# A gated graph network and an attention layer: gates by tanh, scores through DRAM, a product in three float32r passes

## The chip, the core and the metric

The kernel runs on one core of a Trainium2 chip. A core has engines that run their own instruction streams in order and meet at semaphores: TensorE (PE in the profile; its weight loads are PEld), VectorE (DVE), ScalarE (ACT), GpSimd (POOL) and SyncE (SP), which here issues nearly all DMA transfers. The metric is the device time of one execution in microseconds; the time before is the median of five runs.

## The reference

The input x is 64 graphs of 256 nodes with 256 features, adj 64 matrices of 256 x 256. Layer 0 is a gated graph network of three steps, layer 1 a graph attention; each is added to its input.

```python
# layer 0
h = relu(layernorm(x))
A = (adj != 0)
for i in range(3):
    m = h @ weight[i]
    aggr = A.T @ m                       # per graph
    gi, gh = aggr @ w_ih.T + b_ih, h @ w_hh.T + b_hh
    r = sigmoid(i_r + h_r)
    z = sigmoid(i_z + h_z)
    n = tanh(i_n + r * h_n)
    h = (1 - z) * n + z * h
x = x + h
# layer 1
y = relu(layernorm(x))
h = y @ W.T
e = (h @ a_left)[:, :, None] + (h @ a_right)[:, None, :]
e = where(e > 0, e, 0.2 * e)
e = where(adj == 0, -1e9, e)
x = x + softmax(e) @ h
```

All is float32.

## The kernel before

The graphs are worked on in 32 pairs. Most tiles are 128 partitions by 512 elements: one graph's 256 x 256, or one half of the features of both graphs of a pair.

*Setup* (`setup`). The weights are loaded and transposed on TensorE. weight[i] and w_ih are multiplied into one matrix per step. Each factor is cut in two (`factors`, lines 372 to 392): a top part with the low 12 bits of its word masked away (`cut`, line 322, mask -4096), and what is left. Three float32r arrays are kept in `fac`: the top, the remainder times 4096, and a combination (line 387). W^T is kept whole in plain float32 (`wT`). The products a_left W and a_right W are made once (`va`), so that the scores are dot products with y.

*Gates.* The activations are cut in the same way (`split`, lines 445 to 453): a cut on VectorE, a cast on ScalarE (line 449), a difference (line 450) and a combination (line 451) on VectorE. A product is then three float32r passes (`gate`): two in the group "top" (line 464), then ScalarE multiplies the PSUM bank by 1 + 1/4096 ("scale", line 478), then the third pass, "rest" (line 469). Four gate outputs per feature half are made in each step: r (sigmoid, line 599), the h part of n ("nh", with its bias in the scale), its input part ("ni"), and z (sigmoid, line 610). Line 603 is r times nh, line 606 adds ni, line 607 is the tanh, lines 615 to 617 give the new state.

*Between steps.* "prop" (line 584) multiplies by the adjacency in float32r, "prop copy" (line 588) takes it out of PSUM. The state is held transposed; it is turned back by a DMA transpose (line 489) with gathers (line 494), and a copy on ScalarE (`join`, line 502). The last pair does this on TensorE (line 631).

*Attention*, at the end of `pair`. After the second layer norm, line 656 makes the scores with an accumulating scalar_tensor_tensor. The right-hand scores lie one to a partition; TensorE transposes each column, broadcast, so that every partition gets the row of all 256 (line 667, into a PSUM bank). "leaky" (line 671) adds the left-hand score as bias and applies Prelu on ScalarE. A predicated copy (line 674) puts the scores of edges over -1e9, line 676 takes the maximum, and one operation "exps" for both graphs (lines 679 to 687) makes exponentials and their sums. They are transposed (by DMA; the last pair on TensorE, line 700), "mix" (line 714) multiplies y by them in plain float32, "mix copy" (line 718) takes it out, "project" (line 723) multiplies by W^T in plain float32, and line 728 divides by the sums and adds the residual before the store (line 731).

*Order.* Nothing runs as written. `Plan` gathers all operations with a duration (`occ`), a time to the result (`lat`), and what they read and write. `Plan.run` then lays them out one at a time: the one that can start first, ties by a due time (`prio`), moved by the figures in the table `LEAD` (in ns, by operation name). At most four pairs are under way. Buffers come from fixed sets: 28 "full", 32 "round", 12 "small", 8 PSUM "bank". Each engine's queue, SP's with the DMA issues among them, then holds its instructions in that order. The gates' top products take turns (`in_turn`), so that steps of neighbouring pairs alternate.

Of the kernel before, what the change touches and what calls it, by code (L numbers as in the profile page):

```python
# [10 lines left out]
F32 = mybir.dt.float32  # L11
# [16 lines left out]
    "w load": 28000, "w copy": -12000, "w cut": -5000, "w 1": -17000, "w copies": -7000, "G": -9000, "G copy": -5400,  # L28
    "va copy": 4000, "in 0 stats": 5000, "in 1 relu": 10000, "turn copy 0": -11800, "h0 0": 17000, "h0 d": 13000,
    "h1 0": 36000, "prop 0": 11200, "g0 cut": 3000, "g1 cut": 13000, "g1 0": -28000, "r 0 topT": 51000,  # L30
    "r 0 rest": -4300, "r 0": 29000, "ni 0 rest": 46000, "z 0 topF": -48000, "z 0": 11000, "d mul 0": -19000,
    "r 1 topT": -34000, "r 1 rest": -1000, "nh 1 topF": -42000, "nh 1 scale": -38000, "nh 1 rest": 3000,
    "ni 1 topF": -24000, "tanh 1": 10000, "z 1 topF": -61000, "z 1 scale": -112000, "z 1": 6000, "back 0": -36000,
    "hi 0": 28000, "back copy 1": -67000, "hi 1": 52000, "mid 0 stats": -14000, "right 0": -8000,
    "mid 1 eps": -23000, "mid 1 relu": 9000, "dot 1": -31000, "mix 0": -28000, "p copy 1": 40000,
    "project 1": -6000, "turn 1 gather": 2000,
# [16 lines left out]
class Plan:  # L53
# [6 lines left out]
    def __init__(self, window, lead):  # L60
        self.ops, self.slots, self.window, self.pair = [], {}, window, -1
        self.writer, self.readers = {}, {}
        self.due = None
        self.stage = None
        self.lead = lead
        self.keep = {"full": 0, "round": 0}
# [4 lines left out]
    def op(self, name, eng, occ, lat, fn, r=(), w=(), ahead=0, port=False):  # L71
        o = Op()
        o.eng, o.occ, o.lat, o.fn, o.pair, o.seq = eng, occ, lat, fn, self.pair - ahead, len(self.ops)
        o.succs, o.prio, o.end, o.port, o.due = [], None, None, port, self.due
        o.stage, o.name, o.lead = self.stage, name, self.lead.get(name, 0)
        preds, bufs = set(), set()
        for b, ks in r:
            bufs.add(b)
            for k in ks:
                if (b, k) in self.writer:  # L80
                    preds.add(self.writer[b, k])
                self.readers.setdefault((b, k), []).append(o)
        for b, ks in w:
            bufs.add(b)
            for k in ks:
                if (b, k) in self.writer:
                    preds.add(self.writer[b, k])
                preds.update(self.readers.get((b, k), ()))
                self.writer[b, k], self.readers[b, k] = o, []
        preds.discard(o)  # L90
        o.preds, o.wait = list(preds), len(preds)
        for q in preds:
            q.succs.append(o)
        o.bufs = [b for b in bufs if isinstance(b, Buf)]
        for b in o.bufs:
            b.left += 1
        self.ops.append(o)
        return o
# [102 lines left out]
def tile_gated_gnn_then_gat(  # L201
# [34 lines left out]

    nc = tc.nc
    P = 128
# [15 lines left out]
    plan.slot_class("full", [const.tile([P, GN], F32, name=f"full{i}") for i in range(28)])  # L254
# [4 lines left out]
    plan.slot_class("bank", [psum.tile([P, GN], F32, name=f"bank{i}") for i in range(8)])  # L259

# [28 lines left out]
    A512, V512, S512, VP256, C512 = 475, 605, 660, 392, 522  # L289
    CUT = -4096  # L290
# [7 lines left out]
    b_rz = const.tile([P, EB], F32, name="b_rz")  # L298
    b_i = vec[:, 2 * DB : 2 * DB + EB]
# [3 lines left out]
    wT = const.tile([P, DB, D], F32, name="wT")  # L303
# [21 lines left out]
    def setup():  # L325
# [16 lines left out]
        dve("b_rz", 70, lambda: nc.vector.tensor_add(b_rz, b_i, b_h), r=[("vec", ONE)], w=[("b_rz", ONE)])  # L342

# [10 lines left out]
        def transposed(dst, region, blocks):  # L354

            def go_for(c):
# [8 lines left out]
                act("w copy", 140 + n * 110, lambda: nc.scalar.copy(dst(c), pt.t[:, : n * P]), r=[(pt, ONE)], w=[region(c)])  # L365
# [5 lines left out]

        def factors(m, T):

            def one(kb, half):
                f = lambda j: fac[m][:, j, kb, ts(half, H)]
                b, t = T[kb][half], Buf("full")
                src, top = lambda: b.t[:, :H], lambda: t.t[:, :H]
                key = (f"fac{m}", ((kb, half),))
                cut("w cut", top, src, H, [(b, ONE)], [(t, ONE)])
                dve2("w 1", 460, lambda: nc.vector.tensor_sub(src(), src(), top()), r=[(t, ONE)], w=[(b, ONE)])  # L380

                def copies():
                    nc.scalar.copy(f(0), top())
                    nc.scalar.activation(f(1), src(), AF.Copy, scale=SPLIT)

                act("w copies", 800, copies, r=[(b, ONE), (t, ONE)], w=[(f"fac{m}", ((kb, half, 0),))])
                dve2("w d", 510, lambda: nc.vector.scalar_tensor_tensor(f(2), top(), -C, src(), op0=ALU.mult, op1=ALU.add),
                    r=[(b, ONE), (t, ONE)], w=[(f"fac{m}", ((kb, half, 1),))])

            for half in range(2):  # L390
                for kb in range(DB):
                    one(kb, half)
# [4 lines left out]
        def whole(T, blocks):  # L397
            for half in range(2):
                transposed(lambda c, half=half: T[c][half].t[:, :H], lambda c, half=half: (T[c][half], ONE),
                           blocks[3 * half : 3 * half + 3])  # L400
# [4 lines left out]
        whole(whhT, whh_n)  # L405
# [24 lines left out]
        transposed(lambda c: wT[:, c, :], lambda c: ("wT", (c,)), W_n)  # L430
# [11 lines left out]

    WT = [("wT", (0, 1))]
# [11 lines left out]
    def gate(name, e, terms, tops, apart=False, bias=0.0):  # L455
# [22 lines left out]
        act(name + " scale", 575 if "nh" in name else A512, lambda: nc.scalar.activation(bank.t, bank.t, AF.Identity, bias=bias, scale=1.0 + C),  # L478
# [56 lines left out]
    def pair(p):  # L535
        plan.pair = p

# [33 lines left out]
        for i in range(L):  # L571
# [23 lines left out]
            for db in range(DB):  # L595
# [3 lines left out]
                act(f"r {db}", 575, lambda b=r_, k=pr, db=db: nc.scalar.activation(b.t, k.t, AF.Sigmoid, bias=b_rz[:, db : db + 1]),  # L599
                    r=[(pr, ONE), ("b_rz", ONE)], w=[(r_, ONE)])  # L600
                en = 2 * DB + db
                ph = gate(f"nh {db}", en, [("hh", hs)], tops, bias=b_h[:, en : en + 1])
                dve(f"u {db}", V512, lambda u=u, k=ph, b=r_: nc.vector.tensor_mul(u.t, k.t, b.t),  # L603
                    r=[(ph, ONE), (r_, ONE)], w=[(u, ONE)])
# [6 lines left out]
                    b.t, k.t, AF.Sigmoid, bias=b_rz[:, DB + db : DB + db + 1]),  # L611
# [4 lines left out]
                dve2(f"d mul {db}", V512, lambda d=d, b=z_: nc.vector.tensor_mul(d.t, d.t, b.t), r=[(z_, ONE)], w=[(d, ALL)])  # L616
                dve2(f"d add {db}", V512, lambda u=u, d=d: nc.vector.tensor_add(d.t, d.t, u.t), r=[(u, ONE)], w=[(d, ALL)])
# [31 lines left out]
        for g in range(G):  # L649
# [12 lines left out]
            pR = Buf("bank")  # L662

            def right(sm=sm, pR=pR):
                for nb in range(NB):
                    c = 12 + NB + nb
                    nc.tensor.transpose(pR.t[:, ts(nb, P)], sm.t[:, c : c + 1].to_broadcast([P, P]), ident)  # L667

            pe(f"right {g}", 2 * TR, right, r=[(sm, (14, 15))], w=[(pR, ONE)])
            for nb in range(NB):  # L670
                act(f"leaky {g}", 365, lambda b=sc[g], nb=nb, pR=pR, sm=sm: nc.scalar.activation(
                    parts(b)[:, nb, :], pR.t[:, :N], AF.Prelu, bias=sm.t[:, 12 + nb : 13 + nb], alpha=LEAKY_SLOPE),
                    r=[(pR, ONE), (sm, (12 + nb,))], w=[(sc[g], (nb,))])
# [5 lines left out]
        def exps():  # L679
            for g in range(G):  # L680
                s = sms[g].t
                for k in range(NB):
                    nc.scalar.activation(parts(pm_[g])[:, k, :], parts(pm_[g])[:, k, :], AF.Exp, bias=s[:, k : k + 1],  # L683
                                         accum_out=s[:, 4 + k : 5 + k])

        plan.op("exps", "ACT", 4 * 490 + 2600, 4 * 490 + 1300 + 200, exps, r=[(s, ONE) for s in sms],
                w=[(b, ALL) for b in pm_] + [(s, (1,)) for s in sms])

        for g in range(G):
# [28 lines left out]
            act(f"mix copy {g}", A512, lambda ag=ag, pg=pg: nc.scalar.copy(ag.t, pg.t), r=[(pg, ONE)], w=[(ag, ONE)])  # L718

            def project(ag=ag, pv=pv):  # L720
                for ib in range(NB):
                    for db in range(DB):
                        nc.tensor.matmul(pv.t[:, ts(ib, D)], ag.t[:, db * N + ib * P : db * N + (ib + 1) * P],  # L723
                                         wT[:, db, :], start=(db == 0), stop=(db == DB - 1))

            pe(f"project {g}", 4 * MM, project, r=[(ag, ONE)] + WT, w=[(pv, ONE)])
# [41 lines left out]
```

## Time and profile before

| | us |
|---|---|
| median of 5 runs | 2124.22 (2119.61 to 2126.58) |
| the profiled execution | 2124.36 |
| its span in the profile | 2122.6 |

The engines' idle time before groups of their instructions, with what ended most of it, is read from lines such as these (line, engine, operation, shapes, count, then busy time and mean of one in ns, then idle time):

```profile
L607 ACT ACTIVATE full<-full,vec 128x512 f32<-128x512 f32 x192 | 135.6, 723 | 3.6 <-DVE full L606 3.6
L615 DVE TENSOR_TENSOR full<-full,full 128x512 f32<-128x512 f32 x192 | 132.2, 689 | 75.0 <-ACT full L607 71.5
L603 DVE TENSOR_TENSOR full<-bank,full 128x512 f32<-128x512 f32 x192 | 131.7, 686 | 113.5 <-ACT full L599 107.3
```

The 192 are 32 pairs, three steps and two feature halves. A matmul of plain float32 leaves two records. Records of one engine overlap a little, so the cost of one in a row is the distance between starts, and less than its mean. Idle time of an engine that isn't the bottleneck costs nothing.

### The profile page before, as it was taken

The numbers are of one execution on the slowest core, as the hardware profiler recorded it, in microseconds if no ns is written. First come the engines' busy times: TensorE is split into PE (matmuls) and PEld (weight loads), VectorE is DVE, ScalarE is ACT, GpSimd is POOL, SyncE is SP. The second block draws the span as 40 slices with busy tenths as digits, with TensorE's granted clock in tenths as the row PEclk, the third lists the DMA queues.
The fourth block names the chain that finished last, engine by engine and source line by source line (L and its number), as shares of the span: only waits on it lengthen the run. The fifth ranks groups of instructions, "written<-read, shape, count | busy, mean of one in ns | idle before, by whom it ended". The sixth has DMA issues, their size and how long they took to land.

```text
span 2122.6 us, 31090 instructions
## 1 busy us (share of the span) xinstructions
PE 2082.2 (98%) x9737; PEld 1712.0 (81%) x9737; DVE 1779.9 (84%) x4148; ACT 1892.2 (89%) x3255; POOL 142.8 (7%) x198
## 2 busy tenths in 40 slices
PE   8999999999999999999999999999999999999997
PEld 6787888888888888888888888888888888888775
DVE  7788888888888888888888888888888888888775
ACT  7788999999999999998999999999999999999865
POOL 1000000000000000000000000000000000000000
PEclk9999999999999999999999999999999999999998
DMA  3456765556765655766556765556765556665531
GB/s 100 79 101 120 139 119 109 97 112 121 139 117 105 100 115 121 139 118 102 101 115 125 139 118 105 99 115 122 136 119 105 100 113 126 134 118 90 89 58 40
DMA packets 729253, 234.35 MB, mean 110 GB/s; under 512 B 660976, under 2 KB 729088, under 8 KB 729088
## 3 DMA queue, kind: packets, MB, share of 16 engines
q1 hardware_dynamic: 729056, 232.36, 58.3%
q8 instruction: 77, 1.26, 0.3%
q14 instruction: 88, 0.72, 0.1%
q10 hardware_dynamic: 32, 0.01, 0.0%
HBM read 52.96 MB, written 16.78 MB: 33 GB/s over the span
## 4 chain that ended last, share of the span: by engine, by line
PE 82%; ACT 8%; DMA 5%; SPq 3%; DVE 2%; issue 1%; ACTq 0%; DVEq 0%
PE bank L464 41%; PE bank L469 21%; PE bank L584 7%; PE bank L714 6%; PE bank L723 5%; DMA full<-full 4%; SPq L494 3%; ACT full L502 2%; ACT bank L478 1%; ACT round L449 1%; ACT full L683 1%; PE bank L421 1%; PE bank L667 1%; ACT L683 1%; ACT full L588 0%
## 5 line engine op out<-in xcount | busy, mean ns | idle before, releaser
L464 PE MATMUL bank<-round,fac 128*128 128x512 f32 x2304 | 623.6, 399 | 1.9 <-ACT round L449 1.7
L464 PE MATMUL bank<-round,fac_hh 128*128 128x512 f32 x2304 | 617.3, 397 | 3.6 <-ACT round L449 3.6
L464 PEld LDWEIGHTS bank<-round,fac_hh 128*128 128x128 f32 x2304 | 432.6, 189 | 104.6 <-ACT round L449 4.8
L464 PEld LDWEIGHTS bank<-round,fac 128*128 128x128 f32 x2304 | 432.7, 189 | 101.8 <-ACT round L449 2.1
L478 ACT ACTIVATE bank<-bank 128x512 f32<-128x512 f32 x576 | 339.3, 591 | 47.9 <-PE bank L464 43.9
L502 ACT COPY full<-full 128x1024 uint16<-128x1024 uint16 x310 | 363.2, 1172 | 19.9 <-DMA full<-full 15.8
L469 PE MATMUL bank<-round,fac_hh 128*128 128x512 f32 x1152 | 355.6, 398 | 3.8 <-ACT bank L478 3.6
L469 PE MATMUL bank<-round,fac 128*128 128x512 f32 x1152 | 356.2, 395 | 0.6 <-ACT bank L478 0.5
L450 DVE TENSOR_TENSOR round<-full,full 128x512 fp32r<-128x512 f32 x384 | 255.2, 684 | 1.7
L469 PEld LDWEIGHTS bank<-round,fac 128*128 128x128 f32 x1152 | 214.5, 188 | 50.9 <-ACT bank L478 2.8
L469 PEld LDWEIGHTS bank<-round,fac_hh 128*128 128x128 f32 x1152 | 208.3, 189 | 57.8 <-ACT bank L478 17.5
L451 DVE SCALAR_TENSOR_TENSOR round<-round,full 128x512 fp32r<-128x512 f32 x384 | 252.2, 682 | 0.9 <-PE bank L464 0.5
L449 ACT CAST round<-full 128x512 fp32r<-128x512 f32 x384 | 239.1, 630 | 8.6 <-DVE full L322 5.6
L603 DVE TENSOR_TENSOR full<-bank,full 128x512 f32<-128x512 f32 x192 | 131.7, 686 | 113.5 <-ACT full L599 107.3
L524 POOL TENSOR_TENSOR small<-small,nhalf 128x2 f32<-128x2 f32 x128 | 106.1, 838 | 1787.3 <-DVE small L522 1784.9
L584 PEld LDWEIGHTS bank<-round,round 128*128 128x128 f32 x1536 | 205.8, 190 | 17.7 <-DVE round L642 2.7
L584 PE MATMUL bank<-round,round 128*128 128x256 f32 x1536 | 216.7, 287 | 3.4 <-DVE round L642 2.0
L610 ACT ACTIVATE full<-bank,b_rz 128x512 f32<-128x512 f32 x192 | 131.7, 687 | 89.2 <-PE bank L469 89.1
L615 DVE TENSOR_TENSOR full<-full,full 128x512 f32<-128x512 f32 x192 | 132.2, 689 | 75.0 <-ACT full L607 71.5
L322 DVE TENSOR_SCALAR full<-full 128x512 int32<-128x512 int32 (+1 forms) x400 | 163.7, 418 | 17.3 <-ACT full L588 8.8
L616 DVE TENSOR_TENSOR full<-full,full 128x512 f32<-128x512 f32 x192 | 131.8, 688 | 43.0 <-ACT full L610 42.3
L607 ACT ACTIVATE full<-full,vec 128x512 f32<-128x512 f32 x192 | 135.6, 723 | 3.6 <-DVE full L606 3.6
(78 smaller groups left out, 2397.4 us busy)
## 6 DMA issues: line engine op xcount, KB each, us to landing
full<-full SPq DMA_DIRECT2D x496, 128.0 KB, 3.5
x<-in_x_dram SPq DMA_DIRECT2D x64, 256.0 KB, 3.3
adj<-in_adj_dram SPq DMA_DIRECT2D x64, 256.0 KB, 3.1
full<-in_x_dram SPq DMA_DIRECT2D x64, 256.0 KB, 3.3
out_dram<-full SPq DMA_DIRECT2D x64, 256.0 KB, 2.7
full<-full SPq DMA_DIRECT2D x248, 64.0 KB, 2.2
full<-full SPq DMA_TRANSPOSE x310, 3.1
full<-in_L_gnn_w_ih_dram SPq DMA_DIRECT2D x3, 256.0 KB, 3.0
```

What stands on the lines that cost most here:

```text
L322: dve2(name, 60 + n * 0.54, lambda: nc.vector.tensor_scalar(dst().bitcast(I32), src().bitcast(I32), CUT, None, op0=ALU.bitwise_and), r=r, w=w)
L449: act(name + " 0", C512, lambda: nc.scalar.copy(v0.t, t.t), r=[(t, ONE)], w=[(v0, ONE)])
L450: dve2(name + " 1", V512, lambda: nc.vector.tensor_sub(v1.t, v.t, t.t), r=[(v, ALL), (t, ONE)], w=[(v1, ONE)])
L451: dve2(name + " d", V512, lambda: nc.vector.scalar_tensor_tensor(vd.t, v1.t.bitcast(F32), -SPLIT, t.t, op0=ALU.mult, op1=ALU.add), r=[(v1, ...
L464: nc.tensor.matmul(bank.t, f(m, j, kb), b.t, start=(first and n == 0), stop=True, skip_group_check=True)
L469: nc.tensor.matmul(bank.t, f(m, 2, kb), s[kb][2].t, start=False, stop=True, skip_group_check=True)
L478: act(name + " scale", 575 if "nh" in name else A512, lambda: nc.scalar.activation(bank.t, bank.t, AF.Identity, bias=bias, scale=1.0 + C), ...
L502: act(name, 1065, lambda: nc.scalar.copy(dst.t.bitcast(U16).rearrange("p (j n b) -> p j n b", j=2, b=2), src.t.bitcast(U16).rearrange(f"p ...
L584: nc.tensor.matmul(pa.t[:, ts(g, N)], b, parts(A[g])[:, sb, :], start=(n == 0), stop=(n == len(terms) - 1))
L607: act(f"tanh {db}", 615, lambda u=u, en=en: nc.scalar.activation(u.t, u.t, AF.Tanh, bias=b_i[:, en : en + 1]), r=[("vec", ONE)], w=[(u, ONE)])
L615: dve2(f"d sub {db}", V512, lambda u=u, d=d: nc.vector.tensor_sub(d.t, d.t, u.t), r=[(u, ONE)], w=[(d, ALL)])
L616: dve2(f"d mul {db}", V512, lambda d=d, b=z_: nc.vector.tensor_mul(d.t, d.t, b.t), r=[(z_, ONE)], w=[(d, ALL)])
```

## The change

Three parts of the computation are done in another way, and the order is laid out anew with them.

- r and z are made by tanh: sigmoid(v) = (1 + tanh(v/2))/2. The halves go into the weights (the n block of w_hh is halved at setup, with its bias `b_nh`), the scale of the activation (0.5) and `b_rz`. The u product and the last two operations of the state become scalar_tensor_tensor operations.
- The right-hand scores, in all pairs but the last, are written to a row in DRAM and read back to all partitions by two DMAs that SP issues. leaky then reads them from SBUF with a stride of two elements.
- project is made in three float32r passes, with W^T in factors and the mixed activations split as for the gates.

The exps become one operation per graph, there are 26 "full" buffers in place of 28, and `LEAD` has new figures, some for the first or the last pair only.

```diff
     def __init__(self, window, lead):
...
+        self.prefix = ""
...
-        o.stage, o.name, o.lead = self.stage, name, self.lead.get(name, 0)
+        o.stage, o.name, o.lead = self.stage, self.prefix + name, self.lead.get(name, 0)
+        if self.prefix:
+            o.lead += self.lead.get(o.name, 0)
...
-    plan.slot_class("full", [const.tile([P, GN], F32, name=f"full{i}") for i in range(28)])
+    plan.slot_class("full", [const.tile([P, GN], F32, name=f"full{i}") for i in range(26)])
...
+    dram = ctx.enter_context(tc.tile_pool(name="dram", bufs=1, space=bass.MemoryType.DRAM))
+    plan.slot_class("line", [dram.tile([1, N], F32, name=f"line{i}") for i in range(4)])
...
+    LINE, SPREAD = 7500, 5300
...
-    wT = const.tile([P, DB, D], F32, name="wT")
+    fac["W"] = const.tile([P, 3, DB, D], F32R, name="fac_W")
...
+        dve("b_rz half", 70, lambda: nc.vector.tensor_scalar(b_rz, b_rz, 0.5, None, op0=ALU.mult), w=[("b_rz", ONE)])
+        dve("b_nh", 70, lambda: nc.vector.tensor_scalar(b_nh, b_h[:, 2 * DB :], 0.5, None, op0=ALU.mult), r=[("vec", ONE)], w=[("b_nh", ONE)])
...
-        transposed(lambda c: wT[:, c, :], lambda c: ("wT", (c,)), W_n)
+        w_T = [Buf("full") for _ in range(DB)]
+        transposed(lambda c: w_T[c].t[:, :D], lambda c: (w_T[c], ONE), W_n)
+        for c in range(DB):
+            factor("W", w_T[c], D, lambda j, c=c: fac["W"][:, j, c, :], (c,))
...
-                act(f"r {db}", 575, lambda b=r_, k=pr, db=db: nc.scalar.activation(b.t, k.t, AF.Sigmoid, bias=b_rz[:, db : db + 1]),
+                act(f"r {db}", 575, lambda b=r_, k=pr, db=db: nc.scalar.activation(
+                    b.t, k.t, AF.Tanh, bias=b_rz[:, db : db + 1], scale=0.5),
...
-                dve(f"u {db}", V512, lambda u=u, k=ph, b=r_: nc.vector.tensor_mul(u.t, k.t, b.t),
-                    r=[(ph, ONE), (r_, ONE)], w=[(u, ONE)])
+                dve(f"u {db}", S512, lambda u=u, k=ph, b=r_: nc.vector.scalar_tensor_tensor(
+                    u.t, b.t, 1.0, k.t, op0=ALU.add, op1=ALU.mult), r=[(ph, ONE), (r_, ONE)], w=[(u, ONE)])
...
-                    b.t, k.t, AF.Sigmoid, bias=b_rz[:, DB + db : DB + db + 1]),
+                    b.t, k.t, AF.Tanh, bias=b_rz[:, DB + db : DB + db + 1], scale=0.5),
...
-                dve2(f"d mul {db}", V512, lambda d=d, b=z_: nc.vector.tensor_mul(d.t, d.t, b.t), r=[(z_, ONE)], w=[(d, ALL)])
-                dve2(f"d add {db}", V512, lambda u=u, d=d: nc.vector.tensor_add(d.t, d.t, u.t), r=[(u, ONE)], w=[(d, ALL)])
+                dve2(f"d mul {db}", V512, lambda d=d, b=z_: nc.vector.scalar_tensor_tensor(
+                    d.t, b.t, 1.0, d.t, op0=ALU.add, op1=ALU.mult), r=[(z_, ONE)], w=[(d, ALL)])
+                dve2(f"d add {db}", V512, lambda u=u, d=d: nc.vector.scalar_tensor_tensor(
+                    d.t, d.t, 0.5, u.t, op0=ALU.mult, op1=ALU.add), r=[(u, ONE)], w=[(d, ALL)])
...
+            if p < NPAIR - 1:
+                line, pR = Buf("line"), Buf("full")
+                plan.op(f"line {g}", "SP", 420, LINE, lambda line=line, sm=sm: nc.sync.dma_start(
+                    line.t.rearrange("o (q k) -> (o q) k", k=NB), sm.t[:, 12 + NB : 12 + 2 * NB]),
+                    r=[(sm, (14, 15))], w=[(line, ONE)])
+                plan.op(f"right {g}", "SP", 420, SPREAD, lambda line=line, pR=pR: nc.sync.dma_start(
+                    pR.t[:, :N], line.t.to_broadcast([P, N])), r=[(line, ONE)], w=[(pR, ONE)])
+                pr = lambda pR: pR.t[:, :N].rearrange("p (q k) -> p k q", k=NB)
+            else:
...
             for nb in range(NB):
-                act(f"leaky {g}", 365, lambda b=sc[g], nb=nb, pR=pR, sm=sm: nc.scalar.activation(
-                    parts(b)[:, nb, :], pR.t[:, :N], AF.Prelu, bias=sm.t[:, 12 + nb : 13 + nb], alpha=LEAKY_SLOPE),
-                    r=[(pR, ONE), (sm, (12 + nb,))], w=[(sc[g], (nb,))])
+                act(f"leaky {g}", 365, lambda b=sc[g], nb=nb, pR=pR, sm=sm, pr=pr: nc.scalar.activation(
+                    parts(b)[:, nb, :].rearrange("p (k q) -> p k q", k=NB), pr(pR), AF.Prelu, bias=sm.t[:, 12 + nb : 13 + nb],
+                    alpha=LEAKY_SLOPE), r=[(pR, ONE), (sm, (12 + nb,))], w=[(sc[g], (nb,))])
...
-        def exps():
-            for g in range(G):
-                s = sms[g].t
+        for g in range(G):
+            def exps(s=sms[g], m=pm_[g]):
...
-        plan.op("exps", "ACT", 4 * 490 + 2600, 4 * 490 + 1300 + 200, exps, r=[(s, ONE) for s in sms],
-                w=[(b, ALL) for b in pm_] + [(s, (1,)) for s in sms])
+            act(f"exps {g}", 2 * 497, exps, r=[(sms[g], ONE)], w=[(pm_[g], ALL), (sms[g], (1,))])
...
-            def project(ag=ag, pv=pv):
-                for ib in range(NB):
-                    for db in range(DB):
-                        nc.tensor.matmul(pv.t[:, ts(ib, D)], ag.t[:, db * N + ib * P : db * N + (ib + 1) * P],
-                                         wT[:, db, :], start=(db == 0), stop=(db == DB - 1))
-
-            pe(f"project {g}", 4 * MM, project, r=[(ag, ONE)] + WT, w=[(pv, ONE)])
+            cs = split(f"c{g}", ag)
+
+            def project(js, first, cs=cs, pv=pv):
+                for n, (ib, db, j) in enumerate((ib, db, j) for ib in range(NB) for db in range(DB) for j in js):
+                    nc.tensor.matmul(pv.t[:, ts(ib, D)], cs[j].t[:, db * N + ib * P : db * N + (ib + 1) * P],
+                                     fac["W"][:, j, db, :], start=(first and n == 0), stop=True, skip_group_check=True)
+
+            pe(f"project {g}", 8 * PROP, lambda project=project: project((0, 1), True),
+               r=[(cs[0], ONE), (cs[1], ONE), ("facW", ((0, 0), (1, 0)))], w=[(pv, ONE)])
+            act(f"project {g} scale", A512, lambda pv=pv: nc.scalar.activation(pv.t, pv.t, AF.Copy, scale=1.0 + C), w=[(pv, ONE)])
+            pe(f"project {g} rest", 4 * PROP, lambda project=project: project((2,), False),
+               r=[(cs[2], ONE), ("facW", ((0, 1), (1, 1)))], w=[(pv, ONE)])
```

`factor` is the body of `factors` as a function of its own, with the same four operations; it now serves W^T too. `transposed` gets a width up to which it copies, and multiplies the rest by 0.5.

## The prediction

> **What bounds the kernel now.** I read the head of the page first: which engine is never free.
>
> ```profile
> span 2122.6 us, 31090 instructions
> PE 2082.2 (98%) x9737; PEld 1712.0 (81%) x9737; DVE 1779.9 (84%) x4148; ACT 1892.2 (89%) x3255; POOL 142.8 (7%) x198
> ...
> PE 82%; ACT 8%; DMA 5%; SPq 3%; DVE 2%; issue 1%; ACTq 0%; DVEq 0%
> ```
>
> The chain of waits is four fifths TensorE. A busy share can flatter TensorE, because overlapping matmuls are modelled, so I asked next for TensorE's waits between 200 and 1900 us, where start and end of the program play no part (waited for; us in all, times, longest):
>
> ```profile
> PE bank L714 <- ACT full L502: 6.2, 11, 1.2
> PE bank L469 <- ACT bank L478: 0.9, 3, 0.4
> ```
>
> 7.1 us of waiting in 1700. The chain shows line 723 starting at 1576.79 and again at 1640.06, one pair of graphs later, so a pair takes about 63.4 us. One such stretch in the table of windows (PE, PEld, DVE, ACT, POOL busy, clock, DMA share):
>
> ```profile
> 200.00:263.40 63.40, 63.09 (x299) 51.99 (x298) 54.64 (x128) 58.17 (x100) 4.48 (x6) 1.00 0.62 114
> ```
>
> TensorE has 0.3 us free of 63.4, ACT 5.2 and DVE 8.8, at full clock. So in the steady part time is TensorE's own work, and what leaves its queue is gained as long as ACT and DVE still keep up. The last view is TensorE's timeline, for the real price of each kind of matmul (start, length; records overlap, so only distances between starts count):
>
> ```profile
> 1596.40 2.06 PE L584 MATMUL bank<-round,round 128*128 128x256 f32 x16
> 1598.31 0.62 PE L469 MATMUL bank<-round,fac_hh 128*128 128x512 f32 x2
> ...
> 1616.00 0.60 PE L667 MATMUL bank<-ident,small 128*128 128x128 f32 x4
> 1616.35 1.17 PE L464 MATMUL bank<-round,fac 128*128 128x512 f32 x4
> 1617.36 1.10 PE L469 MATMUL bank<-round,fac_hh 128*128 128x512 f32 x4
> ...
> 1639.89 3.62 PE L723 MATMUL bank<-wT,full 128*128 128x256 f32 x16
> 1643.16 2.21 PE L464 MATMUL bank<-round,fac 128*128 128x512 f32 x8
> ```
>
> Line 584 is a float32r product of 128x128 by 128x256, the form that the new product has: 16 in 1.91 us, 119 ns each; elsewhere 8 took 0.94 us, 118 each. Line 723, the plain float32 product with W^T, leaves two records for each product: 16 records for a pair, 3.27 us to the next start, and the next group of 8 takes 0.18 us longer than its usual 8 x 0.233 (after the project at 1576.62 it took 2.05), so 3.45 in all, as the chain also has it. The right-hand scores (line 667) take 0.35 us and make the next group 0.08 longer: 0.43 per pair.
>
> **Part 1, product with W^T.** Per graph 1.725 us of TensorE become 12 matmuls (8 top, 4 rest) x 0.1185 = 1.42: 0.303 less, x 62 graphs = **-18.8 us**; the last pair is costed with the end.
> What it adds per graph lies on other engines. DVE: a cut (line 322), a difference (L450) and a combination (L451), 420 + 684 + 682 ns as records, some 1.55 us between starts, where two L450 in a row take 1.29. ACT: a cast (L449), 0.52 between starts, and a scale (L478), 0.51. So 3.1 us of DVE and 2.06 of ACT per pair.
>
> A rule of the Trainium skill speaks against this part. Perfetto Trace Analysis, in its opening note, calls matmul busy time a bad measure and LDWEIGHTS busy the good one; that is 81% here, and the product with W^T goes from 16 weight loads a pair to 24, less 4 for the scores. Were loads the limit at their recorded 190 ns, that would be 4 x 0.19 x 31 = 24 us slower, near 2148 us. The row disagrees: line 584's loads are recorded at 190 ns too, and its matmuls still follow each other at 119. I go by the row.
>
> **Part 2, right-hand scores.** Four transposes a pair leave TensorE in 31 pairs: 31 x 0.43 = **-13.3 us**. In their place SP issues two DMAs a graph, a line out to DRAM and a spread back, where the second waits for the first to land. The trace has no such small DMA; its nearest are the 64 KB gather (2.2 us to landing) and the store to DRAM (2.7), so leaky starts 4 to 6 us later. Leaky, mask, max and exps of that graph are late by it, and 8 or so buffers of the pair are held so much longer. SP's issues in the pair from 1576 us add up to about 32 of 63 us; four more at some 0.6 are 2.4. A spread that waits at the head of SP's queue holds back the transposes (L489) and gathers (L494) behind it, for whom the back copy and then prop (L584) wait. Lower bound nothing; upper, every spread blocking 2.7 us that reaches TensorE, 62 x 2.7 = 167. I take nothing: SP already stands 564.8 us in its transposes waiting for L617, so it has spare time, and SP's order is made in the plan with the landings in it. If that cover is gone, PE's wait for L502 grows first.
>
> **Part 3, gates by tanh.** TensorE's queue is untouched. ACT loses its table loads (groups and ACT's timeline):
>
> ```profile
> L683 ACT ACT_TABLE_LOAD x32 | 41.1, 1283 | 0.6
> L599 ACT ACT_TABLE_LOAD x31 | 39.8, 1283 | 1.4 <-PE bank L469 0.9
> ```
> ```profile
> 1047.40 1.28 ACT L683 ACT_TABLE_LOAD   x1
> 1048.70 0.51 ACT L683 ACTIVATE full<-full,small 128x256 f32<-128x256 f32 x1
> ...
> 1052.93 0.71 ACT L607 ACTIVATE full<-full,vec 128x512 f32<-128x512 f32 x1
> ...
> 1055.82 1.28 ACT L599 ACT_TABLE_LOAD   x1
> ```
>
> Tanh (L607) ran straight after the exps, and the load came only for the sigmoid: tanh and exp share a table. So two loads a pair go, 2.57 us and about 0.2 of lost overlap. All in shade: ACT had 5.2 us free. Sigmoid to tanh costs 0 to 34 ns (L599 689, L607 723), at 12 a pair at most 0.4. Leaky reads SBUF with a stride instead of PSUM: between its own 477 and the 592 of L530 from SBUF, 0 to 0.46 a pair. On DVE, the u product becomes a scalar_tensor_tensor that reads PSUM: 0 if like L451 (682 against 686), up to 59 ns (L728's 477 against L638's 418 at 256 wide), 0.35 a pair; d mul and d add stay, by L451.
>
> ScalarE: Activation LUTs, section "What ACT_TABLE_LOAD costs", puts a switch at 2.66 us with its drain. The trace shows 1.28 and the exp 20 ns after it, so ACT gains 2.8 a pair and not 5.3; either way nothing of it is in the sum.
>
> ACT after: 58.17 - 2.77 + 2.06 = 57.5 us of a period of 63.4 - 0.61 - 0.43 = 62.4: 92%, as now. DVE: 54.64 + 3.1 = 57.7, with the u product 58.0: 93%, where it had 86. Nearer than before, but not the bound.
>
> **New waits in the steady part.** The split (mix copy, cut, difference) puts some 2 us between mix and project that weren't there, and the scale comes before the rest. Below: nothing, if gates lie between, as with the gates' own splits, which have the same form and cost no wait from 200 to 1900 us. Far bound: all of it exposed, 62 x 3 = 186. Nearest is the row of L714's own wait, 6.2 us; I take half of it, **+3.5**, with 13 (twice) as top of the likely. The 26 buffers in place of 28 are in this too.
>
> **End and start.** At the end nothing covers the split: last mix copy, then 0.42 + 0.68 + 8 x 0.12 + 0.6 + 4 x 0.12 and hand-overs, 3.4 in all, against 1.73 of project: **+2** (1 to 3.5, as the clock falls to 0.85 there). The end's load of exp's table gains nothing: exp waited for max anyway. At the start the load before the first r (36.98 us) cost TensorE about 1 us in L469; W's factors add four small operations per half on ACT and DVE: **-0.5** (-1 to +2).
>
> **Sum.** The profiled execution took 2124.4 (span 2122.6 and 1.8 around it), 0.1 from the median of 2124.22. 2124.4 - 18.8 - 13.3 + 3.5 + 2 - 0.5 = **2097 us**. Bounds of the terms and the spread of the runs: 2090 to 2112.
>
> **Rivals.**
> *Part of it is given back:* ACT and DVE, both over 90%, make every second split or join late by the mean wait of the L714 row (6.2/11 = 0.56 us): two per graph, 64 x 0.56 = 36 less what is counted; at half that, 2097 + 18 = 2115. For it: the only steady wait there is comes from ACT. Against: ACT gets no fuller.
> *DVE becomes the bound (slower):* its place is L603, L615 and L616, which wait in order for r, tanh and z, 88.9 + 64.3 + 31.8 us in 1700, 6.9 a pair. If these can't be filled, a pair takes 58.0 + 6.9 = 64.9, 1.5 more than now: 2124 + 31 x 1.5 + 2 = 2172. It decides once DVE must keep more than 5.4 us of its 8.8 idle. Against: these waits are those of an engine ahead of TensorE, and shrink when work is put in.
> *The loads don't go:* nothing in the trace shows Prelu (leaky) in exp's table. If it isn't, and exps of the two graphs now stand apart, there are up to four loads a pair: ACT 57.5 + 4 x 1.38 = 63.0, with half its old idle time 65.6: 2124 + 31 x 2.2 = 2192. With two, 60.3 of 62.4, some 2107. Against: copies (L449, L502) and Identity (L478) run between the exps and the next load.
>
> **How the numbers follow.** Forecast 0.66, part given back 0.13, DVE 0.15, loads 0.06 (a quarter of it with two). A run tells 0.2%, about 4 us, from no change. Faster: 0.66 + 0.13 + 0.015, less 0.025 for what comes near the old time: 0.78; same 0.03; slower 0.19. The range runs from 2089 through the second case and the lightest part of the DVE case, where all but 0.13 us a pair of its price is filled (2124 + 31 x 0.13 + 2): 2130.
>
> **What would show it.** Per pair 62.4 us between starts of project; 24 project matmuls at 118 to 120 ns; one table load in all; TensorE's steady waits below 13 us; DVE some 93%. Wrong if TensorE waits above 0.5 us a pair (for whom tells which rival), if the new matmuls go over 140 ns, or if loads stand before leaky.

## The result and the profile after

| | before | after |
|---|---|---|
| median, us | 2123.97 (45 runs) | 2125.48 (25 runs, 2121.83 to 2130.51) |
| ratio | | 1.0009 (95%: 1.0003 to 1.0016) |
| profiled execution / its span | 2124.36 / 2122.6 | 2126.41 / 2124.6 |

Forecast was 2097, in 2089 to 2130. The time lies in the range, but the gain of 27 us didn't come: the change costs 0.1% instead. The head of the page and the shares of the chain of waits, after:

```profile
span 2124.6 us, 32372 instructions
PE 2062.7 (97%) x9869; PEld 1683.1 (79%) x9869; DVE 1889.2 (89%) x4348; ACT 1889.7 (89%) x3325; POOL 144.7 (7%) x198
...
PE 64%; ACT 14%; DMA 10%; DVE 6%; issue 4%; SPq 2%; ACTq 0%; DVEq 0%
```

TensorE was 82% of the chain and is 64%; ACT and DMA together went from 13% to 24%. TensorE's busy time fell by 19.5 us, the span did not. Its waits from 200 to 1900 us, which were 7.1 us in all:

```profile
PE bank L492 <- ACT bank L501: 13.5, 17, 1.3
PE bank L750 <- ACT full L525: 8.3, 12, 2.1
PE bank L608 <- DVE round L669: 5.4, 10, 1.1
PE bank L608 <- ACT round L668: 0.5, 1, 0.5
```

(L492 is rest, L501 scale, L750 mix, L525 the join after a DMA turn, L608 prop, L669 lo; after the change they have these lines.) Waits shorter than the overlap of the records don't show here. So I added up TensorE's distances between starts, took the median distance of each form as its price (232 ns for 128x512 in float32r, 119 for 128x256, 216 for a record of plain float32, 109 for a transpose) and call the rest loss:

| us | priced work, whole run | loss 0 to 200 | loss 200 to 1900 | loss after 1900 |
|---|---|---|---|---|
| before | 2047.4 | 22.8 | 18.0 | 24.8 |
| after | 2015.8 | 20.0 | 57.1 | 22.5 |

The work left TensorE as forecast: -31.6 us, where the sum had -32.1. The start and the end are no worse. All of it is lost again in the steady part, where the loss grew by 39 us.

The parts did what they should. Project in the timeline after, where 8 float32r matmuls take 0.96 us to the next start:

```profile
1596.12 1.12 PE L760 MATMUL bank<-fac_W,round 128*128 128x256 f32 x8
1597.08 1.10 PE L487 MATMUL bank<-round,fac 128*128 128x512 f32 x4
```

And the only table load of the whole run, in the groups by line and form:

```profile
L384 ACT ACT_TABLE_LOAD x1 | 1.3, 1283 | 2.0 <-issue 2.0
```

One place shows the new loss from end to end. SP's queue, then ACT's and TensorE's timeline of the changed kernel, a few lines of each:

```profile
1138.35 1.12 SPq L325 DMA_DIRECT2D adj<-in_adj_dram  x2
1139.57 1.28 SPq L517 DMA_DIRECT2D full<-full  x2
```
```profile
1143.61 0.59 ACT L612 COPY full<-bank 128x512 f32<-128x512 f32 x1
1145.84 1.16 ACT L525 COPY full<-full 128x1024 uint16<-128x1024 uint16 x1 [1.64 <-DMA full<-full]
```
```profile
1145.10 0.82 PE L492 MATMUL bank<-round,fac_hh 128*128 128x512 f32 x2
1147.05 1.99 PE L750 MATMUL bank<-full,full 128*128 128x256 f32 x8 [1.13 <-ACT full L525]
```

Two loads of adj, 512 KB together, are issued just ahead of a gather (the second graph's transposed exponentials). The chain of waits shows how long the second half of the gather then takes:

```profile
1140.22 5.54 DMA full<-full
```

This is one of the slower ones. Over pairs 3 to 28 the second half of that gather takes 4.4 us in the median, where all transfers of its form have 3.3 in the list of DMA issues. ACT stands 1.64 us at the join, mix 1.13. In the order before, no load stood between those gathers; that gather was no quicker there (5.2 us in the median, behind four other gather transfers of 128 KB), but its join waited less: 360 ns in the mean from 200 to 1900 us, against 629 after the change.

### The profile page after: what moved, and what is told of

The parts are those of the page before. It is cut to its first block, busy times and chain, and to the rows that moved or that the text cites. A ratio compares the mean times of both kernels' runs of the same rounds, so it can differ in the third digit from the quotient of the medians.

```text
span 2124.6 us, 32372 instructions
## 1 busy us (share of the span) xinstructions
PE 2062.7 (97%) x9869; PEld 1683.1 (79%) x9869; DVE 1889.2 (89%) x4348; ACT 1889.7 (89%) x3325; POOL 144.7 (7%) x198
## 4 chain that ended last, share of the span: by engine, by line
PE 64%; ACT 14%; DMA 10%; DVE 6%; issue 4%; SPq 2%; ACTq 0%; DVEq 0%
PE bank L487 35%; PE bank L492 17%; DMA full<-full 9%; PE bank L608 5%; PE bank L750 3%; ACT full L525 2%; ACT round L472 2%; ACT bank L501 2%; PE bank L760 2%; ACT full L553 2%; SPq L517 1%; ACT full L623 1%; DVE full L628 1%; ACT full L720 1%; ACT full L754 1%
## 5 line engine op out<-in xcount | busy, mean ns | idle before, releaser
L487 PE MATMUL bank<-round,fac_hh 128*128 128x512 f32 x2304 | 621.7, 398 | 4.2 <-ACT round L472 4.2
L487 PEld LDWEIGHTS bank<-round,fac 128*128 128x128 f32 x2304 | 426.8, 188 | 98.4 <-ACT round L472 1.6
L525 ACT COPY full<-full 128x1024 uint16<-128x1024 uint16 x310 | 361.6, 1166 | 43.8 <-DMA full<-full 40.4
L492 PE MATMUL bank<-round,fac_hh 128*128 128x512 f32 x1152 | 366.0, 403 | 3.7 <-ACT bank L501 3.7
L501 ACT ACTIVATE bank<-bank 128x512 f32<-128x512 f32 x576 | 328.7, 578 | 42.6 <-PE bank L487 40.2
L492 PE MATMUL bank<-round,fac 128*128 128x512 f32 x1152 | 351.3, 398 | 13.2 <-ACT bank L501 13.2
L474 DVE SCALAR_TENSOR_TENSOR round<-round,full 128x512 fp32r<-128x512 f32 x448 | 303.7, 684 | 3.8
L473 DVE TENSOR_TENSOR round<-full,full 128x512 fp32r<-128x512 f32 x448 | 301.8, 685 | 3.7
L472 ACT CAST round<-full 128x512 fp32r<-128x512 f32 x448 | 269.9, 616 | 20.3 <-DVE full L336 20.1
L492 PEld LDWEIGHTS bank<-round,fac 128*128 128x128 f32 x1152 | 211.8, 188 | 76.9 <-ACT bank L501 29.8
L492 PEld LDWEIGHTS bank<-round,fac_hh 128*128 128x128 f32 x1152 | 207.3, 188 | 57.5 <-ACT bank L501 15.6
L336 DVE TENSOR_SCALAR full<-full 128x512 int32<-128x512 int32 (+1 forms) x466 | 194.1, 418 | 51.7 <-ACT full L754 22.6
L608 PEld LDWEIGHTS bank<-round,round 128*128 128x128 f32 x1536 | 207.0, 190 | 22.9 <-DVE round L669 8.0
L608 PE MATMUL bank<-round,round 128*128 128x256 f32 x1536 | 213.8, 285 | 6.0 <-DVE round L669 5.4
L628 DVE SCALAR_TENSOR_TENSOR full<-full,bank 128x512 f32<-128x512 f32 x192 | 131.7, 687 | 90.6 <-PE bank L492 43.3
L635 ACT ACTIVATE full<-bank,b_rz 128x512 f32<-128x512 f32 x192 | 131.8, 686 | 17.1 <-PE bank L492 11.5
L623 ACT ACTIVATE full<-bank,b_rz 128x512 f32<-128x512 f32 x192 | 130.5, 682 | 17.0 <-PE bank L492 13.2
L641 DVE SCALAR_TENSOR_TENSOR full<-full,full 128x512 f32<-128x512 f32 x192 | 130.7, 681 | 16.5 <-ACT full L635 16.4
```

The costliest lines, as they stand in the source:

```text
L336: dve2(name, 60 + n * 0.54, lambda: nc.vector.tensor_scalar(dst().bitcast(I32), src().bitcast(I32), CUT, None, op0=ALU.bitwise_and), r=r, w=w)
L472: act(name + " 0", C512, lambda: nc.scalar.copy(v0.t, t.t), r=[(t, ONE)], w=[(v0, ONE)])
L473: dve2(name + " 1", V512, lambda: nc.vector.tensor_sub(v1.t, v.t, t.t), r=[(v, ALL), (t, ONE)], w=[(v1, ONE)])
L474: dve2(name + " d", V512, lambda: nc.vector.scalar_tensor_tensor(vd.t, v1.t.bitcast(F32), -SPLIT, t.t, op0=ALU.mult, op1=ALU.add), r=[(v1, ...
L487: nc.tensor.matmul(bank.t, f(m, j, kb), b.t, start=(first and n == 0), stop=True, skip_group_check=True)
L492: nc.tensor.matmul(bank.t, f(m, 2, kb), s[kb][2].t, start=False, stop=True, skip_group_check=True)
```

## The experiments

Three runs (b4, d1, d2) start from the kernel before, all others from the changed kernel. All keep the plan of the kernel they start from, with its durations, its figures and so its order on every engine, and alter only what single operations do, or where DMA issues stand. To undo a part and lay the order out anew would have mixed the part with another order. Times are medians of 4 to 10 runs; the ratio, with its 95% interval, is to the kernel before, run beside them. The code cuts show the lines that matter, shortened.

**1. Which engine pays? One relief at a time.** The line and spread DMAs are left out (a fixed row is read), or the DVE work of project's split, or the ACT work that the three passes add:

```diff
# a1: no DMAs through DRAM
-    lambda line=line, sm=sm: nc.sync.dma_start(...)
-    lambda line=line, pR=pR: nc.sync.dma_start(...)
+    lambda: None      # both
+    pr = lambda pR: va[:, 0, :].rearrange("p (q k) -> p k q", k=NB)
# a2: no cut, difference, combination; a3: no cast, no scale
+    cs = split(f"c{g}", ag, True)     # the fn of these operations is None
```

> The changed kernel with every queue in the same order, but the two DMAs a graph through DRAM are not issued; leaky reads a fixed row of the same shape and stride in their place (so the attention's right-hand scores are left out). If SP's queue and the landing of line and spread are what makes the joins late (25 of the 39 us of new TensorE stalls between 200 and 1900 us sit before L492 and L750, whose ACT work stands behind late joins), it falls by 20 us or more, to about 2100, and ACT's wait for DMA in the joins goes back from 35 us toward 10. If DVE's or ACT's added work is the cause, it stays within 5 us of 2125.

> The changed kernel in the same order, with the three DVE operations of project's split left out (3.1 us of DVE a pair); the cast reads the mixed activations directly and all passes read it, so the product with W^T is not the right one. If the fuller DVE is the cause, 20 us or more are regained: about 2100 and TensorE's waits between 200 and 1900 us down from 28 us toward 10. If it is SP and the DMAs, it stays within 5 us of 2125. If the order simply has no slack anywhere, each such relief gains a part, 5 to 15 us.

> The changed kernel in the same order, with the two ACT operations that the three passes add left out (the cast of the top half and the scale, 2.06 us of ACT a pair); the product with W^T then lacks its top half. If ACT is the cause, 20 us or more are regained, to about 2100, the waits of L492 for L501 first. If DVE or SP is, within 5 us of 2125. If no single engine is, 5 to 15 us.

Measured 2127.71 (ratio to before 1.0016, 1.0006 to 1.0026), 2122.38 (0.9989, 0.9978 to 1.0) and 2123.04 (0.9999, 0.9988 to 1.0011). The changed kernel has 2125.48. So the round trip through DRAM costs nothing; 3.1 us of DVE a pair are worth some 3 us in all, 2.06 of ACT some 2. None of the three is the cause of the 39 us.

**2. The loads.** x for the first norm and adj loaded for the first pair only, first in the changed kernel, then in the one before, and then with the same issues but an eighth of the bytes (the x loads of the residual stay):

```diff
-    dma("load", 256, lambda: nc.sync.dma_start(parts(b), rows(src, g)), ...
+    # a4, b4
+    dma("load", 256, lambda: nc.sync.dma_start(parts(b), rows(src, g)) if g < G or cls == "full" else None, ...
+    # a7
+    ... else nc.sync.dma_start(parts(b)[:, :, :32], rows(src, g)[:, :, :32]), ...
```

> The changed kernel in the same order, but x (for the first norm) and adj are loaded for the first pair only, and all pairs work on those; four of the six 256 KB loads of a pair and their SP issues go, line and spread stay. If late DMAs are the cause through traffic or through SP's issue time at large, it falls by 15 us or more; if the cause is only the wait of spread for line inside SP's queue, it stays within 8 us of 2125 while the run without line and spread falls.

> The kernel before, in its own order, with x (for the first norm) and adj loaded for the first pair only, as was done to the changed kernel, which gained 21 us by it. If late DMAs are what the change newly pays for, the kernel before, with 18 us of TensorE stalls from 200 to 1900 us, can gain little: 2 to 8 us. If the loads cost any kernel of this form 20 us, it gains 15 or more and the DMAs are no reason for the difference.

> The changed kernel in the same order; the loads of x and adj after the first pair are issued as before by SP with the same waits, but bring an eighth of the bytes (32 of 256 columns), so all pairs work on mostly old data. If the traffic of the loads in the DMA engines is what makes joins late, it falls as without the loads, to about 2105. If it is SP's queue (their issue time, and their waits for a free buffer in front of transposes and gathers), it stays near 2125.

Changed kernel without the loads: 2104.45 (0.9907, 0.9892 to 0.9922). The kernel before without them: 2124.88 (1.0009, 0.9998 to 1.002), nothing. The changed kernel with small loads: 2106.4 (0.9924, 0.9909 to 0.9939). So the loads' bytes cost the changed kernel some 20 us and the one before nothing, and in the changed kernel SP's issue time and its waits for a free buffer are not the main reason. Of the ten joins of a pair, in order of time, the eighth, which releases the second graph's mix, waited 629 ns in the mean from 200 to 1900 us after the change, 25 with the small loads and 0 without (the expectation of the first swap, below, has 658 and 31).

**3. The same loads by GpSimd's queue.**

```diff
-    nc.sync.dma_start(parts(b), rows(src, g))
+    nc.gpsimd.dma_start(parts(b), rows(src, g))
```

> The changed kernel in the same order, all loads of x and adj (the residual's too) issued by GpSimd instead of SP, with nothing left out: the same bytes, but SP has six issues a pair less. If SP's queue is the cause, some 15 to 25 us are regained, to 2100 to 2110. If it is traffic, it stays within 5 us of 2125; slower only if GpSimd's own queue, where the pow of the norms stands behind a load that waits for its buffer, becomes late.

Measured 2202.25 (1.0372, 1.0349 to 1.0396). The bytes stay and the time grows. GpSimd's queue has the small operations of the norms and the fills, and a load now stands ahead of them, waiting for its buffer. How that lateness reaches TensorE was not followed. GpSimd's waits from 200 to 1900 us, whose first number is the sum in us:

```profile
POOL full L325 <- DVE round L474: 337.7, 20, 17.2
```

**4. The place.** Two swaps in SP's queue of the changed kernel, everything computed. In the first only the two adj loads of a pair move, behind the gather that follows them (28 of the 31 pairs have them there); in the second every load and store that stands ahead of a gather moves behind it:

```diff
# c1, in Plan.run
+            elif o.name.endswith("load") and (held or last_sp.endswith("p turn 0 gather")):
+                held.append(o)      # issued after "p turn 1 gather"
# c2
+            if o.eng == "SP" and o.pair >= 0 and o.name.endswith(("load", "store")):
+                held.append(o)      # issued after the gathers that come next
```

> The changed kernel, everything computed; in SP's queue alone, the two adj loads of a pair (512 KB) that stand between the two p turn gathers go behind the second. If what the join before mix waits for (658 ns in the mean, 0 to 31 without the loads' bytes) is these two loads ahead of its gather, most of the 19 to 21 us that the small or missing loads gave is regained by this swap alone: 2108 to 2113, and TensorE's loss in front of mix goes from 16 us in 1700 to below 5. If it is the loads' traffic wherever it stands, it stays within 4 us of 2125.

> The changed kernel, everything computed; in SP's queue alone, all loads and stores that stand ahead of a gather go behind it (the adj loads, the residual's x loads, the two stores between the turn gathers). If it is places ahead of gathers that cost, it gains at least as much as the swap of the adj loads: 2103 to 2111. If bunching loads and stores behind the gathers only moves the delay to the next transposes, it is no better than the swap, or worse.

The swap alone gives 2106.66 (0.9925, 0.9908 to 0.9942), as much as leaving the bytes out. SP's queue after it, and TensorE's waits:

```profile
1064.61 3.44 SPq L534 DMA_DIRECT2D full<-full  x4
1068.10 1.16 SPq L342 DMA_DIRECT2D adj<-in_adj_dram  x2
```
```profile
PE bank L509 <- ACT bank L518: 13.4, 17, 1.3
PE bank L625 <- DVE round L686: 5.3, 8, 1.2
PE bank L767 <- ACT full L542: 1.2, 5, 0.4
PE bank L625 <- ACT round L685: 0.5, 1, 0.5
```

The wait in front of mix (now L767) went from 8.3 to 1.2 us; its loss, by distances, from 16.3 to 2.8. The waits for scale (L518) are as they were. The second swap is slower than either kernel: 2142.8 (1.0091, 1.0076 to 1.0106). There the wait has moved, to prop:

```profile
PE bank L623 <- DVE round L684: 37.5, 26, 2.9
PE bank L507 <- ACT bank L516: 1.9, 6, 0.4
```

The chain of waits leads to one of them:

```profile
1151.13 4.29 DMA full<-full
...
1155.52 0.70 DVE full L643
...
1157.64 0.69 DVE round L684
...
1158.37 0.98 PE bank L623 x6
```

The DMA is the transpose of the first graph's exponentials, which SP now issues behind two x loads. u (L643) of another pair gets the buffer that this transpose reads (so the plan has it in 28 pairs), and lo (L684), which prop needs, stands behind u in DVE's queue. From 200 to 1900 us u waits 59.9 us for DMAs in this run and 24.8 in the changed kernel (where it is L628):

```profile
DVE full L643 <- DMA full<-full: 59.9, 26, 3.7
```

The waits for scale (here L507 for L516) are nearly gone in it, which was the hint for step 6.

**5. The same place in the kernel before.** Two copies of 255 KB a pair from DRAM to DRAM, read by nobody, ahead of that gather, or behind it:

```diff
+            if name.endswith("p turn 1"):
+                for k in range(2):
+                    nc.sync.dma_start(spare[k][:, :255], adj[k][:, :255])
             for q in range(2):
                 nc.sync.dma_start(dst(slice(64 * q, 64 * q + 64)), view(q, blocks))
```

> The kernel before, all computed, with two further copies of 256 KB a pair (adj to a row store in DRAM that nobody reads) just ahead of the second p turn gather, where the changed kernel has its adj loads. If a place ahead of that gather is what costs, the kernel before gets slower by 8 to 25 us, with mix waiting for the join. If the kernel before has the slack for it, within 4 us.

> The same two copies just behind that gather: the same bytes and SP issues. By the theory of place, clearly less than the other, 0 to 6 us over the kernel before; by a theory of SP's issue time or of traffic at large, as slow as the other.

Ahead: 2146.33 (1.0107, 1.0087 to 1.0127). Behind: 2125.2 (1.0012, 1.0002 to 1.0022). The same bytes and issues differ by 21 us through their place alone. TensorE's longest waits in the two, ahead first:

```profile
PE bank L719 <- ACT full L507: 20.8, 23, 2.3
```
```profile
PE bank L719 <- ACT full L507: 9.2, 15, 2.3
```

A place ahead can delay the gather in two ways: SP issues it later, or it lands later once issued. The trace tells them apart. Times are counted from the landing of the transpose of the second graph's exponentials, as medians of pairs 3 to 28; the last column is the mean wait of the join from 200 to 1900 us:

| us | its gather is issued | it has landed | ACT waits at the join |
|---|---|---|---|
| before | 0.74 | 6.54 | 0.36 |
| copies ahead (d1) | 2.00 | 7.10 | 1.02 |
| copies behind (d2) | 0.73 | 6.42 | 0.48 |
| after | 0.62 | 6.03 | 0.63 |
| small loads (a7) | 0.61 | 4.85 | 0.03 |
| adj loads behind (c1) | 0.08 | 4.55 | 0.00 |

In the kernel before it is the issue: 1.27 us later, and landed 0.68 later, which over 31 pairs makes 21 us. In the changed kernel it is mostly the bytes: with the same issue, 1.18 us less with small loads. So d1 and d2 show that the place costs, and a7 that bytes do; the order before had no margin at this join either.

**6. The 10 us that were still missing.** On the first swap (2106.66): the two stores between the turn gathers go behind them, and the two x loads there behind the next back gather; or no stores; or no DMAs through DRAM; or no DVE work in project's split:

```diff
# c3, on c1
+            if o.eng == "SP" and o.name.endswith("store"):
+                stores.append(o)     # issued behind the last turn gather
+            elif o.eng == "SP" and after_turn and o.name.endswith("load"):
+                parted.append(o)     # issued after "back 1 gather"
# c4, on c1
-    nc.sync.dma_start(rows(out, G * p + g), parts(b)), r=[(XR[g], ALL)])
+    nc.sync.dma_start(rows(out, G * p + g), parts(b)) if p >= NPAIR - 2 else None, r=[(XR[g], ALL)])
# c5: c1 with a1; c6: c1 with a2
```

> The changed kernel with the adj loads behind the p turn gathers (2106.7 us), everything computed; further, the two stores between the turn gathers go behind them and the two x loads there behind the next back 1 gather, so that as many bytes as before stand ahead of back 1. If the remaining waits of rest for scale (L492, 23 us of loss in 1700 against 5 before the change) come from joins of the turn gathers that stand behind stores, it gains a further 5 to 12 us: 2095 to 2102. If they are of ACT's order itself, within 4 us of 2106.7; slower, if back 1 becomes late as it did when all loads and stores yielded.

> The changed kernel with the adj loads behind the p turn gathers, and without the stores of all pairs but the last two (their output is left out). By the theory of traffic ahead of the turn gathers, 2095 to 2102; by the theory that ACT's order has no slack there, within 4 us of 2106.7.

> The changed kernel with the adj loads behind the p turn gathers, and without the two DMAs a graph through DRAM (leaky reads a fixed row, the right-hand scores are left out). With the adj loads in the way these DMAs cost nothing (2127.7 without, 2125.5 with). If they were only hidden behind that stall, 4 to 10 us are gained now; if the round trip through DRAM is free, within 4 us of 2106.7.

> The changed kernel with the adj loads behind the p turn gathers, and without the three DVE operations of project's split (all passes read the cast of the mixed activations; the product with W^T is not the right one). If the fuller DVE is what still keeps 10 us of the forecast gain, 6 to 12 us are gained, to 2095 to 2101; if not, within 4 us of 2106.7.

Measured: 2092.79 (0.986, 0.9845 to 0.9874), 2095.29 (0.987, 0.9855 to 0.9884), 2108.84 (0.9936, 0.992 to 0.9953), 2101.03 (0.9903, 0.9888 to 0.9918). With the stores moved, all is computed and the gain is even larger than forecast for this run. Its waits and its window from 200 to 1900 us (PE, PEld, DVE, ACT, POOL busy, clock, DMA share, GB/s):

```profile
PE bank L644 <- DVE round L705: 5.0, 8, 0.9
PE bank L786 <- ACT full L561: 1.4, 5, 0.6
PE bank L528 <- ACT bank L537: 0.8, 3, 0.5
```
```profile
200.00:1900.00 1700.00, 1692.66 (x8208) 1400.07 (x8207) 1568.07 (x3618) 1574.57 (x2757) 123.94 (x162) 1.00 0.61 122
```

The waits of rest for scale (L528 for L537) fell from 13.5 to 0.8 us, although scale itself was never touched: ACT runs in order, and scale stood behind joins that waited for gathers behind stores. The two joins after the turn gathers waited 218 and 349 ns in the mean after the change, 46 and 0 in c3 (0 and 82 before). That the run without stores, with the x loads in place, gains nearly as much puts it down to the stores. TensorE is busy for 1692.66 us, and DVE for 1568 and ACT for 1575 (92 and 93%), more than in the changed kernel, without holding it up. Without its split DVE gives 5.6 us, between what the two expectations said; how much of that is DVE and how much the shorter way from mix to project stays open.

| loss of TensorE from 200 to 1900, us | L492 rest | mix | prop | all | time |
|---|---|---|---|---|---|
| before | 5.0 | 11.2 | -0.6 | 18.0 | 2124.0 |
| after | 24.3 | 16.3 | 9.1 | 57.1 | 2125.5 |
| adj loads behind (c1) | 23.2 | 2.8 | 8.4 | 39.8 | 2106.7 |
| and stores, x loads (c3) | 6.9 | 3.1 | 7.1 | 22.8 | 2092.8 |

("all" has the other lines too.) In c3 the priced work is 2015.8 us, as after the change, and the loss of the whole run 65.2, where before it was 65.6: the 32 us are kept in full. It still has the tanh gates, the 26 buffers and one exps per graph, so none of these is the cause.

## Why the prediction was wrong

*What bounds the kernel:* right. TensorE's work sets the time wherever the transfers stand well, and each microsecond of it taken away is gained (c3).

*Part 1 and part 2, TensorE:* right, -31.6 for -32.1. Had weight loads been the limit, as the prediction read the opening note of Perfetto Trace Analysis in the Trainium skill (which names MFU beside them), the new project would have been dearer; its 24 loads a pair are recorded at 188 ns and its matmuls follow at 119 in the median, so the row held.

*Part 2, SP and DRAM:* right that the round trip is free, shown twice (a1, c5): no gain without it, some 2 us slower each time, which is within the noise. No run speaks against the spare time of SP as the cover for its issues; the sentence beside it, that the plan has the landings in it, is where the failed step begins.

*Part 3:* right that the loads go. There is one table load, so Prelu too is in the table that the run keeps, and the rival "the loads don't go" falls. That nothing of ACT's gain shows in the time was not tested by itself.

*ACT and DVE near 92%:* forecast busy for 92% and 93%, measured 1544.8 and 1540.4 us in 1700, 91%. Both rivals that rest on them fall, by a2, a3 and c3. The case "part of it is given back" had the right place, the joins, and the wrong reason.

*New waits in the steady part, +3.5, 13 at most of the likely:* this is the step that failed. It measured 39, and TensorE's waits were 1.05 us a pair, where the prediction called itself wrong above 0.5. I sized it by one row of the old order, L714's own wait, as if the waits hung on what the parts add to each engine. They hang on what stands ahead of what in SP's queue, against the moment at which ACT comes to the join. The new figures in `LEAD` got no term; I noted only that "SP's order is made in the plan with the landings in it". But the plan counts a fixed landing for each transfer (4300 ns for this gather, in the code of `dma_turn`), whatever is queued ahead; from its first issue it measured 5.1 us in the median after the change and 5.9 before. With the new figures the plan put two adj loads ahead of one gather and two stores among the turn gathers. With those four moved, and two x loads, the waits are back where they were. The order before has no load or store at these places, and without its loads it gains nothing. Its joins were not free of waits (360 ns at the second graph's exponentials), but at the second turn gather's join ACT came 3.1 us after the landing, in the median; after the change it came 0.1 us before it, and in c3 1.2 after.

*The period:* the two starts of line 723 that the prediction quotes lie 63.27 us apart, not 63.4, and the mean from 200 to 1900 us is 63.8. It was to fall to 62.4; it rose to 64.3 and is 63.0 in c3.

*End and start, +2 and -0.5:* TensorE's loss fell by 2.3 us after 1900 us and by 2.8 before 200. The table load that is gone at the start may be one reason; I did not take this apart.

*The range:* that the time lies in it is luck. Its upper part, to 2130, stood for the first two rivals, and the reasons that these give are not what happened.

Shown, then: the gain of the parts is real, and was given back through the place of a few transfers a pair, two adj loads and two stores (c3 also moves two x loads). Not shown: which single figure of `LEAD` put them there, and whether another order would do as well as c3.

## What to carry to other kernels

When a change comes with a new order, read the transfer queue as closely as the engines: list what stands ahead of each transfer that an in-order engine waits for, count its bytes and its issues, and ask when that engine comes to wait. A planner with a fixed time for each transfer can't see that a bulk load delays a small gather behind it, so let bulk loads and stores give way to gathers, but not all at once: here, with all of them moved, the delay went to the next transpose (2142.8 us). To tell a part from its order, keep the order and change what single operations do.

## What the runs showed of the hardware

- Two copies (510 KB) cost 21 us more ahead of a gather than behind it (2146.3 against 2125.2, 31 pairs, 0.68 us a pair), with the DMA engines busy for 61% and 65% of the time only. There the gather was issued 1.27 us later. Behind two loads of 256 KB a gather landed 6.03 us after its transpose, behind loads of an eighth of the bytes, issued alike, 4.85.
- A late join on ACT shows as a wait for another operation, scale, and on TensorE's side for rest (13.5 us, 0.8 with the stores moved): the releaser named there had no share in the cause.
- A load issued by GpSimd took 4.3 to 4.4 us to land, by SP 3.2 to 3.5, and blocked what GpSimd had behind it: loads waited 337.7 us there for one line of DVE alone.
